# Weights laid out with the summed dimension first, a prologue without transposes, and x loaded by quarters

## The chip, the cores and the metric

The kernel runs on one NeuronCore of a Trainium2 chip. The core has five engines with a queue of instructions each: TensorE (PE in the profile; its weight loads are listed apart as PEld), VectorE (DVE), ScalarE (ACT), GpSimd (POOL) and SyncE (SP). They work side by side and wait for each other by semaphores. PE reads SBUF and writes PSUM; DMA moves data between HBM and SBUF. The metric is the device time of one execution in microseconds, median of several runs. Before the change it was 1078.87 us (three runs, 1078.11 to 1079.22).

## What is computed

```python
w = weights[conditions]                       # (128, 64, 64), one matrix for each of 128 samples
x1 = einsum('bct,bcd->bdt', x, w)             # x is (128, 64, 512)
h  = gelu(x1 @ ternarize(W1).T + b1)          # W1 is (2048, 512)
y  = h @ ternarize(W2).T + b2                 # W2 is (512, 2048)
scale = max(|y|) / 7 + 1e-8                   # over the whole tensor
out = x + clip(round(y / scale), -7, 7) * scale

def ternarize(W):
    delta = 0.05 * max(|W|)
    mask = |W| > delta
    return sum(|W| where mask) / max(sum(mask), 1) * sign(W) * mask
```

All arrays are float32, except for the conditions, which are integers.

## The kernel before

The 128 samples make 16 blocks (n = 0 to 15) of eight samples, that is 512 columns (samples times channels). Each block goes through two layers of 16 steps (hc = 0 to 15), one step for each 128 of the 2048 hidden units.

A block's input comes from "condition": the eight gathered 64x64 matrices stand in pairs on the diagonals of four 128x128 tiles ("diag"), and PE multiplies a pair of samples of x by each (`mix`, into PSUM tile "pc"). To keep float32 accuracy, a value is stored as a high and a low part, both in the format fp32r (`split`: ACT copies the high part, DVE or POOL subtracts to get the low one), and every product is made with both. The weights are ternary, -1, 0 or 1, so one part is enough. They are kept as fp8 in "w1t" and "w2t", and POOL widens 128x512 of them to fp32r ("wf") just ahead of use (`widen1`, `widen2`).

A step of layer 1 (`layer1`) is eight products of 128x512 into PSUM tile "ph". `bend` has ACT apply Gelu with scale alpha into a "ring" tile and splits the result into "h". A step of layer 2 (`layer2`) is eight products into the four PSUM tiles "py", which sum over all 16 steps. `result` then scales by the second alpha and keeps y in SBUF, and `largest` takes the maximum of it.

Blocks 2 to 11 (`SEVEN`) make layer 1 of two steps together with seven products of half size in place of eight (`seven`, driven by `pair`; weights combined once into "w1s"). `condition7` prepares their inputs with five intermediate results in a scratch tile "mixed". The other blocks go by `eight`. x of the next block is loaded on SP's queue: two DMAs of 512 KB into a "big" tile, at the first pair or step of the block ahead.

The prologue (block 0, and all that comes before) has to find the thresholds. In nat1 and nat2 the weights lie as they come from HBM, with the hidden unit or output channel on the partitions, so that the summed dimension lies along the row. DVE takes the maxima of W1, group by group (four groups of four steps), as they arrive. ACT makes signs and magnitudes. From the threshold on, DVE makes mask and sign of each group (`mask1`, `signed1`), and PE turns the ternary tiles (`turn1`, `turn2`: eight transposes of 128x128 in bf16 for two steps, into PSUM tile "pt"), ACT or DVE casts the result to fp8 into w1t or w2t, and POOL widens from there. `count1` counts the masks by products with a tile of ones, `alpha_1` joins the sums. Layer 1 of block 0 starts before alpha is known: `early` makes the products into five rotating PSUM tiles, `early_bend` follows four steps behind. Layer 2 of block 0 follows after all of its layer 1, and in between the four mixes of block 1. Fifty-two products of ones ("idle") keep PE busy until the first threshold.

Every engine runs its instructions in the order in which the program writes them (class `InOrder`); nothing rearranges them. Tiles come from pools: "big" has 20 tiles of 8 KB for each partition, "half" 10 of 4 KB. A tile that takes the place of another waits until that one's last reader is done.

At the end, when the maximum of all y is known, x is loaded once more, y is rounded, added to x and written out.

All lines of the kernel are recorded as line 54 in the profile (the class `InOrder` makes each instruction), so groups are told apart by their tiles' names.

Of the kernel before, what the change touches and what calls it, by code (L numbers as in the profile page):

```python
# [38 lines left out]
P = 128  # L40
# [17 lines left out]
def tile_cond_ternary_ffn(  # L58
# [17 lines left out]
    H = W1.shape[0]  # L76
    assert 2 * C == P and 2 * D == P and W1.shape[1] == T and C == D

    NT = T // P
    NH = H // P  # L80
# [7 lines left out]
    SEVEN = range(2, 12)  # L88
# [36 lines left out]
    first = big.tile([P, 5, max(B, P)], F32, tag="big", name="first")  # L125
    cond_i = first[:, 0, :B].bitcast(I32)
    sp.dma_start(out=cond_i, in_=conditions.partition_broadcast(P))
# [4 lines left out]
    PIECES.append([slice(0, 2), slice(2, 3), slice(3, GH)])  # L132
    for g in range(NG):
        w = big.tile([P, GH, T], F32, tag="big", name=f"nat1_{g}")
        rows1 = W1[g * GH * P : (g + 1) * GH * P, :].rearrange("(k p) t -> p k t", p=P)
        for ks in PIECES[g]:
            sp.dma_start(out=w[:, ks, :], in_=rows1[:, ks, :])
        nat1.append(w)
    x_next = load_x(0)
    b1n = first[:NH, 4, :P]  # L140
    sp.dma_start(out=b1n, in_=b1.rearrange("(k p) -> k p", p=P))
    for g in range(NG):
        w = big.tile([P, NT, GH * P], F32, tag="big", name=f"nat2_{g}")
        sp.dma_start(
            out=w,
            in_=W2[:, g * GH * P : (g + 1) * GH * P].rearrange("(i p) h -> p i h", p=P),
        )
        nat2.append(w)
# [4 lines left out]
    ident_b = const.tile([P, P], BF16)  # L153
    make_identity(nc, ident_b)
    ident_f = const.tile([P, P], F32)
    make_identity(nc, ident_f)
    ones_b = const.tile([P, P], BF16)
    pool.memset(ones_b, 1.0)
    ones_f = const.tile([P, P], F32)
    pool.memset(ones_f, 1.0)  # L160

# [8 lines left out]
    cond_f = first[:, 1, :B]  # L170
    dve.tensor_copy(cond_f, cond_i)
    wrap = first[:, 2, :B]
# [3 lines left out]
    cond_2 = cond_f.rearrange("p (j two) -> p j two", two=2)  # L176
# [4 lines left out]
    for h in range(2):  # L181
        dve.tensor_scalar(
            rows[half_of(h), :],
            cond_2[half_of(h), :, h],
            float(C),
            chan_f[half_of(h), :],
            ALU.mult,
            ALU.add,
        )
# [31 lines left out]
    def mix(xt, j, pc):  # L221

        for c in range(NT):
            pe.matmul(
                out=pc[:, c, :],
                lhsT=xt[j // 2][:, j % 2, c * P : (c + 1) * P],
                rhs=diag[:, j, :],
                start=True,
                stop=True,
            )  # L230

    def condition(n, j, xt, two):
        pc = ps_c.tile([P, NT, P], F32, tag="pc", name=f"pc_{n}_{j}")
        mix(xt, j, pc)
        split(pc, *(t[:, :, j * P : (j + 1) * P] for t in two))


    w1t = big.tile([P, NH, NT, P], F8, tag="big", name="w1t")
    w1t_f = w1t.rearrange("p h c k -> p h (c k)")
    w2t = big.tile([P, NH, T], F8, tag="big", name="w2t")  # L240

# [28 lines left out]
    def turn(dst, src, name):  # L270

        pt = ps_c.tile([P, len(src), NT, P], BF16, tag="pc", name=f"pt_{name}")
        for i, tiles in enumerate(src):
            for c, t in enumerate(tiles):
                pe.transpose(pt[:, i, c, :], t, ident_b)
        return lambda engine, dst=dst, i=slice(0, len(src)): (
            engine.copy(dst, pt[:, i], saturate=False)
            if engine is act
            else engine.tensor_copy(dst, pt[:, i], saturate=False)
        )  # L280

    def turn1(g, i, sign):

        hc = g * GH + 2 * i
        return turn(
            w1t[:, hc : hc + 2],
            [
                [sign[:, (2 * i + k) * T + c * P :][:, :P] for c in range(NT)]
                for k in range(2)
            ],  # L290
            f"1_{g}_{i}",
        )

    def turn2(g, i, sign):
        hc = g * GH + 2 * i
        return turn(
            w2t[:, hc : hc + 2].rearrange("p k (c d) -> p k c d", c=NT),
            [
                [sign[:, c * GH * P + (2 * i + k) * P :][:, :P] for c in range(NT)]
                for k in range(2)  # L300
            ],
            f"2_{g}_{i}",
        )

# [4 lines left out]
    signs = [big.tile([P, 2, WCH], BF16, tag="big", name=f"signs_{i}") for i in range(2)]  # L309
    junk = big.tile([P, 2, WCH], BF16, tag="big", name="junk")  # L310
# [3 lines left out]

    def sign1(g):
        act.activation(signs[g // 2][:, g % 2, :], flat(nat1[g]), AF.Sign)
# [14 lines left out]
    for _ in range(52):  # L331
        pe.matmul(out=idle, lhsT=ones_b, rhs=above[:, :T], start=True, stop=True)
# [17 lines left out]
    fetched = [fetch(1, j) for j in range(PAIRS)]  # L350
# [3 lines left out]
    def mix0(j):  # L354
        pc = ps_y.tile([P, NT, P], F32, tag=f"py{j}", name=f"pc_0_{j}")
        mix(x_next, j, pc)
# [14 lines left out]
    mix0(0)  # L371
    mix0(1)
    hi0(0)
    hi0(1)
    tern1 = {}

    def mask1(g, part=slice(0, WCH)):

        if g not in tern1:
            tern1[g] = big.tile([P, 2, WCH], BF16, tag="big", name=f"tern1_{g}")  # L380
        dve.tensor_scalar(
            tern1[g][:, 0, part], flat(mags[g])[:, part], delta1, None, ALU.is_gt
        )

    def signed1(g, part=slice(0, WCH)):
        both = tern1[g]
        dve.tensor_tensor(
            both[:, 1, part], both[:, 0, part], signs[g // 2][:, g % 2, part], ALU.mult
        )

    def count1(g, number, first, final):
        for i in range(WCH // T):
# [3 lines left out]
                rhs=tern1[g][:, 0, i * T : (i + 1) * T],  # L396
                start=(first and i == 0),
                stop=(final and i == WCH // T - 1),
# [9 lines left out]
    mask1(0, parts1[0])  # L408
    signed1(0, parts1[0])
    turned = turn1(0, 0, tern1[0][:, 1, :])  # L410
    lo0(0)
    lo0(1)
    mix0(2)
    mix0(3)
    pb = ps_c.tile([P, NH], F32, tag="pc", name="pb")
    pe.transpose(pb, b1n, ident_f[:NH, :NH])
    b1t = const.tile([P, NH], F32)
    wf1 = [half.tile([P, 2, NT, P], F32R, tag="half", name=f"wf1_{i}") for i in range(2)]
    w1f = [wf1[i // 2][:, i % 2] for i in range(4)]
    turned(act, w1f[0], 0)  # L420
    hi0(2)
    hi0(3)
    turned(act)
    sign1(3)
    lo0(2)
    lo0(3)
    mask1(0, parts1[1])
    signed1(0, parts1[1])
    dve.tensor_copy(b1t, pb)
# [4 lines left out]
    wide1 = {(0, 0): w1f[0]}  # L434
# [7 lines left out]
    def widen1(n, hc):  # L442

        w = w1f[hc % 4] if n == 0 else w1f[hc % 2]
        pool.tensor_copy(w, w1t[:, hc])
        wide1[n, hc] = w

    def widen2(n, hc):
# [7 lines left out]
        pool.tensor_copy(w, w2t[:, hc])  # L456
        wide2[n, hc] = w

    def layer1(n, hc, ph, pieces=1):

        w = wide1.pop((n, hc))
        for i in range(pieces):
            part = slice(i * BLK // pieces, (i + 1) * BLK // pieces)
            for c in range(NT):
                for k in range(2):
# [55 lines left out]
    rings = [half.tile([P, 2, BLK], F32, tag="half", name=f"ring_{i}") for i in range(2)]  # L521
    ring = [rings[i // 2][:, i % 2, :] for i in range(4)]

    def early(hc):
# [6 lines left out]
        layer1(0, hc, ph, 2 if hc == 0 else 1)  # L531
        waiting[hc] = ph

    def early_bend(hc):
        if hc % 2 == 0:
            pairs0[hc // 2] = big.tile([P, 2, 2, BLK], F32R, tag="big", name=f"h_{hc}")
        h = pairs0[hc // 2]
        bend(
            0,
            hc,  # L540
            waiting.pop(hc),
            [h[:, hc % 2, k, :] for k in range(2)],
            ring[hc % 4],
            pool if hc in (0, 2, 4, 6, 8, 12, 14) else dve,
        )

    def alpha_1():

        total = ps_c.tile([P, NG], F32, tag="pc", name="total1")
        pe.matmul(out=total, lhsT=ones_f, rhs=sums1, start=True, stop=True)  # L550
        count = const.tile([P, 1], F32, name="count1")
# [555 lines left out]
```

## Time and profile before

| what | us |
|---|---|
| median of three runs | 1078.87 |
| the profiled execution | 1079.13 |
| its span on the chip | 1077.4 |
| PE busy | 999.9 (93%) |
| PEld busy | 867.2 (80%) |
| DVE busy | 594.8 (55%) |
| ACT busy | 598.6 (56%) |
| POOL busy | 613.8 (57%) |
| first threshold known, first mask starts | 18.94 |
| alpha of W1 known, first Gelu starts | 40.78 |
| first product of layer 2 of block 0 | 67.6 |
| first product of block 1 | 100.64 |
| first block by seven products starts | about 163.8 |
| block 12 (eight products) starts | about 761.3 |

The span is the time between the first and the last instruction that the profiler recorded; the execution as timed is 1.7 us longer. A group's row gives engine, operation, tiles written and read, shape, and count, then busy time and mean duration of one in ns, then the engine's idle time ahead of these instructions and what ended it. A row of the timeline gives start, duration (of several merged instructions where "xN" says so), engine and operation, and in brackets the idle time before it. "PEclk" is the clock that TensorE was granted, as a share of full speed.

### The profile page before, as it was taken

How to read it: one execution, taken by the hardware profiler on the slowest of the kernel's cores; microseconds unless marked ns; L12 is line 12 of the kernel's file. 1: busy time of each engine (PE TensorE's matmuls, PEld its weight loads, DVE VectorE, ACT ScalarE, POOL GpSimd, SP SyncE). 2: the span in 40 equal slices, each digit the busy share in tenths (PEclk: the TensorE clock that was granted, in tenths of full speed). 3: DMA queues.
4: the chain of work that ended last, by engine and by line, in shares of the span. 5: the costliest groups of instructions: out<-in, count | busy, mean ns of one | idle time of the engine just before them, and what ended most of it. 6: DMA issues, size and time to landing. Idle time of an engine off the chain costs nothing.

```text
span 1077.4 us, 16522 instructions
## 1 busy us (share of the span) xinstructions
PE 999.9 (93%) x5778; PEld 867.2 (80%) x5780; DVE 594.8 (55%) x1035; ACT 598.6 (56%) x1010; POOL 613.8 (57%) x996
## 2 busy tenths in 40 slices
PE   7999999999999999999999999999999999999400
PEld 4778788999999999999999999999888888888300
DVE  6985845565665566665656556564423223231692
ACT  6865345666666565656656665665443443433481
POOL 4574836666676757666666667575534435333242
PEclk9999999999999999999999999999999999999855
DMA  9202010010100010010101000100200010041799
GB/s 326 87 17 101 5 40 5 2 43 3 42 4 2 5 41 5 1 44 2 43 4 41 5 1 6 40 5 2 82 2 2 4 40 6 1 145 32 283 413 376
DMA packets 28802, 62.22 MB, mean 58 GB/s; under 512 B 2848, under 2 KB 2992, under 8 KB 28720
## 3 DMA queue, kind: packets, MB, share of 16 engines
q1 hardware_dynamic: 22064, 42.28, 11.4%
q0 software_dynamic: 6656, 18.88, 4.5%
q8 instruction: 47, 0.77, 0.3%
q14 instruction: 35, 0.29, 0.1%
HBM read 44.38 MB, written 16.78 MB: 57 GB/s over the span
## 4 chain that ended last, share of the span: by engine, by line
PE 89%; DMA 5%; DVE 4%; ACT 1%; issue 1%; POOL 0%; SPq 0%; POOLq 0%; DVEq 0%; ACTq 0%
PE py L54 43%; PE ph L54 15%; PE xy L54 14%; PE z L54 11%; PE pc L54 5%; DMA xt<-in_x 3%; DVE top L54 1%; DMA out<-y 1%; DMA nat<-in_L_ffn_W 1%; DVE tern L54 1%; PE pt L54 1%; DVE y L54 0%; DVE h L54 0%; ACT ring L54 0%; ACT diag L54 0%
## 5 line engine op out<-in xcount | busy, mean ns | idle before, releaser
L54 PE MATMUL py<-wf,h 128*128 128x512 f32 x2048 | 530.6, 395 | 1.4 <-ACT h L54 0.7
L54 PEld LDWEIGHTS py<-wf,h 128*128 128x128 f32 x2048 | 366.2, 189 | 67.3 <-DVE y L54 2.3
L54 DVE TENSOR_TENSOR h<-ring,h 128x512 fp32r<-128x512 f32 x249 | 191.8, 771 | 227.9 <-ACT h L54 227.9
L54 POOL CAST wf<-w2t 128x512 fp32r<-128x512 fp8e4 x256 | 185.3, 726 | 176.2 <-PE py L54 160.6
L54 POOL CAST wf<-w1t 128x512 fp32r<-128x512 fp8e4 (+1 forms) x255 | 172.5, 682 | 78.0 <-PE ph L54 57.4
L54 PE MATMUL ph<-x,wf 128*128 128x512 f32 (+1 forms) x776 | 192.4, 391 | 1.8 <-POOL wf L54 0.7
L54 ACT ACTIVATE ring<-ring,b1t,alpha_w 128x512 f32<-128x512 f32 x160 | 131.2, 820 | 88.8 <-DVE ring L54 88.8
L54 POOL CAST wf<-w1s 128x256 fp32r<-128x256 fp8e4 (+1 forms) x240 | 122.2, 514 | 99.4 <-PE xy L54 72.7
L54 ACT ACTIVATE ring<-ph,b1t,alpha_w 128x512 f32<-128x512 f32 x96 | 74.9, 780 | 176.3 <-PE ph L54 174.7
L54 PEld LDWEIGHTS ph<-x,wf 128*128 128x128 f32 x776 | 144.5, 188 | 33.3 <-POOL wf L54 1.3
L54 ACT CAST h<-ring 128x512 fp32r<-128x512 f32 x256 | 158.9, 621 | 8.3
L54 DVE TENSOR_TENSOR ring<-xy,ring 128x256 f32<-128x256 f32 (+1 forms) x160 | 88.3, 552 | 58.9 <-PE xy L54 58.9
L54 PEld LDWEIGHTS xy<-xt,wf 128*128 128x128 f32 x640 | 97.8, 189 | 12.8
L54 PE MATMUL xy<-xb,wf 128*128 128x256 f32 x640 | 101.9, 281 | 0.0
L54 PE MATMUL xy<-xt,wf 128*128 128x256 f32 x640 | 101.7, 282 | 0.0
L54 PEld LDWEIGHTS xy<-xb,wf 128*128 128x128 f32 x640 | 92.7, 190 | 7.1
L54 ACT COPY ring<-xy 128x256 f32<-128x256 f32 x160 | 59.1, 370 | 61.6 <-PE xy L54 61.6
L54 PE MATMUL z<-xt,wf 128*128 128x256 f32 x640 | 89.4, 282 | 0.0
L54 ACT COPY ring<-z 128x512 f32<-128x512 f32 x80 | 47.0, 588 | 66.9 <-DVE h L54 63.7
L54 PEld LDWEIGHTS z<-xt,wf 128*128 128x128 f32 x640 | 82.0, 190 | 0.0
L54 POOL DMA_INDIRECT wg<-in_L_cond_weights,rows x64 | 72.3, 1130 | 13.8 <-issue 5.4
L54 DVE TENSOR_TENSOR xt<-mixed,xt 128x512 fp32r<-128x512 f32 x40 | 30.7, 767 | 81.8 <-ACT xt L54 81.8
(111 smaller groups left out, 825.6 us busy)
## 6 DMA issues: line engine op xcount, KB each, us to landing
xt<-in_x SPq DMA_DIRECT2D x60, 512.0 KB, 5.2
out<-y POOLq DMA_DIRECT2D x30, 512.0 KB, 12.8
nat<-in_L_ffn_W SPq DMA_DIRECT2D x6, 1024.0 KB, 14.7
nat<-in_L_ffn_W SPq DMA_DIRECT2D x3, 512.0 KB, 11.4
wg<-in_L_cond_weights,rows POOLq DMA_INDIRECT x64, 2.6
w1t<-in_x SPq DMA_DIRECT2D x4, 256.0 KB, 2.6
w2t<-in_x SPq DMA_DIRECT2D x4, 256.0 KB, 2.7
out<-xt POOLq DMA_DIRECT2D x2, 512.0 KB, 8.5
```

Of the source, the lines that this page charges most:

```text
L54: return lambda *args, **kw: self._tc.keep_in_program_order(make(*args, **kw))
```

## The change

It does five things. The host hands over W1, W2, b1 and the conditions in another layout (`LAID_OUT`), with the summed dimension on the partitions, so that `turn`, `turn1` and `turn2` with their transposes and casts are gone. The order of the prologue is written anew: block 0's widenings read the ternary bf16 tiles ("terns") directly; w1t and w2t are made later, during layer 2 of block 0, by ACT (`kept`). Six ring tiles in place of two let the low halves of odd steps wait (`low`). x of the blocks by seven, and of the block behind them, comes by quarters of 256 KB into a "half" tile with two places, which `condition7` also uses for its intermediate results. And block 12 goes by seven products too. The load of the conditions moves from SP's queue to ACT's, a first use of Gelu on one column stands ahead of everything on ACT, and there are 54 idle products in place of 52.

```diff
-    SEVEN = range(2, 12)
+    SEVEN = range(2, 13)
...
-    sp.dma_start(out=cond_i, in_=conditions.partition_broadcast(P))
+    act.dma_start(out=cond_i, in_=conditions)
...
-        rows1 = W1[g * GH * P : (g + 1) * GH * P, :].rearrange("(k p) t -> p k t", p=P)
         for ks in PIECES[g]:
-            sp.dma_start(out=w[:, ks, :], in_=rows1[:, ks, :])
+            sp.dma_start(out=w[:, ks, :], in_=W1f[:, g * GH :, :][:, ks, :])
...
+    sp.dma_start(out=b1t, in_=b1)
...
+        sp.dma_start(out=w, in_=W2[:, g * GH : (g + 1) * GH, :])
...
-    def turn(dst, src, name):
...
-                pe.transpose(pt[:, i, c, :], t, ident_b)
...
+        if n == 0:
+            w = w1f[hc % 4]
+            g, i = divmod(hc, GH)
+            pool.tensor_copy(flat(w), group1(terns, g)[:, i * T : (i + 1) * T])
...
+        on_pool = hc % 2 == 0 and hc < NH - 2
+        bend(0, hc, waiting.pop(hc), two, ring[hc % len(ring)], pool if on_pool else None)
...
+    fetched = [fetch(1, 0)]
+    mask1(0, parts1[0])
+    signed1(0, parts1[0])
+    widen1(0, 0)
     widen1(0, 1)
+    lo0(0)
+    lo0(1)
+    hi0(2)
+    hi0(3)
+    lo0(2)
+    lo0(3)
+    fetched += [fetch(1, 1)]
     early(0)
+    early(1)
+    mask1(0, parts1[1])
+    signed1(0, parts1[1])
+    widen1(0, 2)
+    widen1(0, 3)
+    fetched += [fetch(1, j) for j in range(2, PAIRS)]
+    abs1(3)
+    for g in range(NG - 1):
+        above1(g)
+    sign1(3)
...
+    early(3, lambda: next(find, None))
+    signed1(2)
     widen1(0, 5)
     early(4)
     early_bend(0)
+    widen1(0, 6)
...
+    def behind(hc):
+        if 5 <= hc < 5 + NG:
+            largest2(hc - 5)
+        if 6 <= hc < 6 + PAIRS:
+            place(hc - 6, fetched[hc - 6])
+        if hc == 9:
+            signed1(3)
+        if hc == 11:
+            delta.extend(next(find))
+            signed2(0)
+        if hc == 12:
+            low(0, 1)
+            low(0, 3)
+            signed2(1)
         if hc == 14:
+            widen2(0, 0)
         if hc == 15:
+            widen2(0, 1)
...
+        if hc + 2 < NH:
+            widen1(0, hc + 2)
         early_bend(hc - 4)
         behind(hc)
...
+    def kept(t, g, tiles):
+        act.copy(flat(t[:, g * GH : (g + 1) * GH]), group1(tiles, g), saturate=False)
...
+        if hc == 0:
+            signed2(2)
+        if hc == 1:
+            for i in (13, 14, 15):
+                low(0, i)
+        if hc < NG:
+            kept(w1t, hc, terns)
+        if hc == 3:
+            signed2(3)
...
+                count2(g)
+            else:
+                kept(w2t, g, terns2)
+        if hc in (5, 7, 9, 11):
+            j = (hc - 5) // 2
+            condition(1, j, pair_of(x_next, j), two_next)
+            sum2(j)
...
-        t, b12 = extra["t"], extra["b12"]
+        t = xp.rearrange("p (a c d) -> p a c d", a=4, c=2)
+        b12 = t[:, 3]
...
+    def quarter_x(n, j):
+        sp.dma_start(out=extra["x"][:, j % 2, :], in_=x_blk[n][:, j, :])
...
-                    x_next.append(load_x(n + 1))
...
+                if k == 1:
+                    quarter_x(n + 1, 0)
+                    quarter_x(n + 1, 1)
+                if k in (4, 5):
+                    quarter_x(n + 1, k - 2)
...
+LAID_OUT = {
+    "itok_B_1_198": lambda a: a.reshape(-1, 2).T.repeat(P // 2, axis=0),
+    "L0_ffn_W1": lambda a: a.reshape(-1, P, a.shape[1] // P, P).transpose(3, 0, 2, 1),
+    "L0_ffn_b1": lambda a: a.reshape(-1, P).T,
+    "L0_ffn_W2": lambda a: a.reshape(a.shape[0], -1, P).transpose(2, 1, 0),
+}
```

## The prediction

> **What bounds the kernel now.** I read the busy shares first (PE 93%), then the chain that ended last (PE 89% of it), then busy time by stage. Columns: stretch, its length, busy time of PE, PEld, DVE, ACT and POOL with instruction counts, granted PE clock, DMA share, GB/s.
>
> ```profile
> 0.00:20.00 20.00, 15.10 (x68) 7.45 (x69) 12.76 (x21) 12.90 (x8) 9.86 (x28) 1.00 0.90 309
> 20.00:40.00 20.00, 17.91 (x110) 13.50 (x111) 15.46 (x19) 16.25 (x17) 8.87 (x16) 0.91 0.68 246
> 40.00:62.00 22.00, 20.58 (x113) 15.83 (x111) 21.20 (x22) 18.26 (x26) 14.91 (x13) 1.00 0.01 2
> 62.00:73.00 11.00, 10.14 (x65) 8.07 (x64) 8.99 (x8) 9.52 (x14) 8.27 (x8) 1.00 0.01 1
> 73.00:101.00 28.00, 27.70 (x162) 22.80 (x163) 19.68 (x16) 14.69 (x17) 15.41 (x15) 1.00 0.23 83
> 101.00:163.80 62.80, 62.73 (x292) 51.25 (x291) 35.85 (x60) 27.32 (x48) 35.79 (x48) 1.00 0.10 33
> 163.80:223.60 59.80, 59.80 (x386) 54.37 (x386) 35.46 (x75) 34.98 (x69) 39.66 (x68) 1.00 0.01 3
> ...
> 761.30:823.00 61.70, 61.70 (x289) 51.35 (x288) 19.92 (x31) 25.79 (x38) 26.85 (x44) 1.00 0.07 20
> ```
>
> From 101 us on PE is hardly ever idle: a block by seven products lasts 59.8 us (163.8 to 223.6), one by eight with its four mixes 61.7 (block 12). After PE's end near 1010 us comes a tail that the change leaves alone. So two things can move the time: the kind of block 12, and the moment at which block 1 starts on PE, 100.64 us. Ahead of that moment PE has work that it keeps from 18.15 us on: eight mixes of 0.98 (two took 1.96), 16 first products of 1.81, 14 second products of 1.81 and some 4 us of counting, 66 us in 82.5. The rest is transposes, waits and a lowered clock (0.91 in 20 to 40).
>
> **Part 1, the transposes go.** Both matrices arrive with the summed dimension on partitions.
>
> ```profile
> L54 PE MATMUL pt<-ident_b,tern 128*128 128x128 bf16 x128 | 10.2, 224 | 1.1 <-DVE tern L54 1.1
> L54 ACT CAST w2t<-pt 128x1024 fp8e4<-128x1024 bf16 x8 | 8.1, 1010 | 11.0 <-PE pt L54 11.0
> L54 ACT CAST w1t<-pt 128x1024 fp8e4<-128x1024 bf16 x7 | 7.1, 1008 | 2.9 <-PE pt L54 2.9
> ```
>
> Sixteen groups of eight transposes go. A group holds PE for 0.40 us (one starts at 65.27, the next product at 65.67), so 6.4 us of path. The chain transpose, ACT cast, POOL cast becomes one POOL cast from bf16; 16 casts leave ACT's and DVE's queues. Eight ACT casts of 2048 columns come in ("kept"). 512 columns took 0.59, 1024 took 1.01, so some 1.87 each, 15 us, now during the second products, where ACT was busy 14.7 of 28 us. With counts at 1.9 + 0.2 their last starting mix copy is ready at about 91 us by my sum, just ahead of its use. A bf16 to fp32r cast on POOL is not in the trace: between 0.61 (the same from fp8, shortest) and 0.81 (mean of the first weights' casts). I take 0.62, nearest in shape; the upper end is at most 3 us on the path.
>
> **Part 2, the first loads.** The index load leaves SP's queue for ACT's: SP issued it at 0.75 and the first weights at 1.19, so 0.44 us earlier. ACT's wait for the first weights covers its issue (idle 5.8 us). DVE's maxima follow the first arrival without a gap, so the threshold comes near 18.4 instead of 18.9. b1 comes as 64-byte rows; it is used 20 us later, which hides it. The rows of weights are 8 KB long, 32 KB apart; see the slower rival.
>
> **Part 3, alpha.** DVE in its new order from 18.4: mask and sign of half a group (1.6), four low halves (0.69 each, held by ACT's copies until 22.4), so 23.1; other half 1.7; mask and sign of group 1 2.5; two masks 2.6; the masked sum 2.3: 32.2. In this stretch POOL issues four widenings and three gathers, and these take turns with DVE.
>
> ```profile
> 40.59 0.16 DVE L54 TENSOR_TENSOR alpha_w<-kept,count 128x1 f32<-128x1 f32 x1
> 40.78 0.78 ACT L54 ACTIVATE ring<-ph,b1t,alpha_w 128x512 f32<-128x512 f32 x1 [1.50 <-DVE alpha_w L54]
> ...
> 58.72 2.34 DVE L54 SCALAR_TENSOR_TENSOR tern<-nat,delta_w,tern 128x2048 bf16<-128x2048 f32 x1
> 59.09 3.13 POOL L54 TENSOR_TENSOR h<-ring,h 128x512 fp32r<-128x512 f32 x1 [3.44 <-ACT h L54]
> ...
> 60.98 2.80 DVE L54 TENSOR_TENSOR h<-ring,h 128x512 fp32r<-128x512 f32 x2
> ...
> 62.16 2.09 POOL L54 CAST wf<-w1t 128x512 fp32r<-128x512 fp8e4 x2
> ...
> 63.29 2.14 PE L54 MATMUL ph<-x,wf 128*128 128x512 f32 x8 [0.68 <-POOL wf L54]
> ...
> 100.64 1.98 PE L54 MATMUL ph<-x,wf 128*128 128x512 f32 x8
> ```
>
> The POOL subtraction beside DVE's 2.34 us takes 3.13 instead of 1.29: it only works once DVE is done (61.06 + 1.2). The two DVE subtractions behind it take 2.80 instead of 1.4. A gather issued beside a 2.70 us DVE addition (117.46) took 2.84 instead of 1.0. The Trainium skill (SBUF — State Buffer, "SBUF: two separate sides") says that DVE and GpSimd share one pair of ports which the first holds for its whole instruction. The rows agree; what the rule alone forbids is adding only the longest engine. By durations alone alpha would come at 34.4; with turns (three to four POOL operations of 0.6 to 1.0 in between) the sum ends at 35.3, eight small steps bring alpha at 37.4. Before: 40.75. ACT's second table load (1.28 at 38.01) goes too, worth nothing: ACT waited 1.5 for alpha behind it. The total for alpha now sits in the middle of product 3 on PE: up to 1.2 us of wait there.
>
> **Part 4, the first products.** The first Gelu ends at 38.2 and frees the PSUM bank of product 5; PE has finished product 4 at the same time. ACT needs 1.33 us a step (40.78, 42.12, 43.45), PE 1.81, so PE leads. Eleven products make 19.9; product 6 waits 0.7 (its widening stands behind POOL's first subtraction, 38.85 + 1.3 + 0.6 = 40.75), the second threshold's transpose costs 0.35. That would be 59.2. Then from 50.9 DVE's two ternarizations of W2 (1.29 + 2.34 each) and two low halves take turns with POOL's widenings 13 to 15 and two subtractions: the widening of product 15 ends at 58.4, so product 15 ends at 60.2. The first W2 widening stands behind them all: 62.3 if POOL takes the first turn, 64.6 if DVE does. I take 62.3, because POOL is free 0.1 us earlier. Layer 2 of block 0 started at 67.4.
>
> **Part 5, the second products.** 14 of 1.81 and four mixes of 0.9 to 0.98 make 29.1, plus 1 us for turns at widenings 2 and 3: block 1 starts at 92.4, 8.2 us earlier. x of block 1 is loaded once block 0's inputs are dead (about 60); 512 KB took 5.2, its first use is at 74: hidden by six products; if it weren't, at most that load's 5 us.
>
> **Part 6, x by quarters.** Four loads of 256 KB instead of two of 512 on SP's queue. SP now waits inside a block for a quarter's buffer; only later x loads are behind it, and the next are used a block later. The quarter is also condition7's scratch, so it comes free when that pair's split ends.
>
> ```profile
> 257.67 0.74 DVE L54 TENSOR_TENSOR xt<-mixed,xt 128x512 fp32r<-128x512 f32 x1 [2.39 <-ACT xt L54]
> ...
> 258.88 1.06 PE L54 MATMUL pc<-diag,xt 128*128 128x128 f32 x8
> ...
> 266.81 1.06 PE L54 MATMUL pc<-diag,xt 128*128 128x128 f32 x8
> ```
>
> Pair 0's quarter is free at 258.41, pair 2's mix is due at 266.81: 8.4 us, for an issue of 0.4 and a landing of 2.6 (the row of 256 KB loads of x). 5.4 us are left. In block 1 the mixes are 4.5 us apart (132.81, 137.34) and the split ends at 137.53; there 1.4 us are left. Taken at nothing; bounds 0 and 2 us.
>
> **Part 7, block 12 by seven.** 61.7 minus 59.8: 1.9 us, all on PE's path. Its extra vector work lies under PE, as in ten blocks before.
>
> **The sum.** Profiled span 1077.4 - 8.2 - 1.9 = 1067.3; that execution took 1079.1, 1.7 around the span, so 1069.0. The median is 0.3 lower: 1068.8.
>
> **The rivals.**
>
> A. The turns are cheaper than I sum (POOL slips in while DVE waits). Then PE alone counts: alpha at 35.5, layer 2 at 57.5, block 1 at 86.6, 14 us earlier: 1063. For it: three of the waits are mine, not measured. Against: every overlap in the rows above was paid in full. 0.22.
>
> B. The turns cost more: DVE first, widenings of layer 2 also late. Block 1 at 95 to 97, total 1071.5 to 1075. For it: POOL's queue is in order, so one late subtraction holds all widenings. 0.20.
>
> C. Slower than before: the weights come slowly. The Trainium skill (DMA: Bandwidth & Descriptors, "Latency and other measured facts") tells of row pitches at large powers of two: at 512 KiB 207 GB/s. This change makes the pitch of both matrices 32 KB; before, W1 was read in whole megabytes and W2 at a pitch of 8 KB, both at 360 to 410 GB/s. By the rows W1's 4.19 MB take some 11 us, by an estimate at the page's 207 they take 20.3: 9.5 us later for the threshold, and everything behind it; that cancels nearly all of the gain of 10.1. It decides below 200 GB/s; at 150 (28 us) the time would be 1086. 8 KB is the nearer row (two doublings against four), so I take the full rate. Slower: 0.05; a rate that leaves about nothing: 0.03.
>
> D. Quarters arrive late. Price: two late quarters in each of 11 blocks. A landing of 8 us instead of 2.6 would be needed to begin with. The DMA share in those blocks is 0.01 to 0.1. It would need 0.5 us each to cancel the gain. Under 0.01.
>
> **How the numbers follow.** Mine 0.50, 1066 to 1071.5; A 0.22; B 0.20; C 0.08. Cases of one sign hold most; the range runs from 1063 (A) to 1075 (B). Faster by over 0.2% (2.2 us, about what a measurement of this kernel can tell from no change) 0.92, within 0.03, slower 0.05.
>
> **What would show it.** No transposes in the list; alpha near 37.4; product 15 ending near 60; the first py product near 62; block 1 near 92; every seven-product block still 59.8 with no PE wait on x; block 12 at 59.8; the rate in the first 25 us near 390 GB/s. I am wrong if the first weights land after 9 us, if POOL's casts from bf16 take over 0.9, or if PE waits for a quarter.

## The result and the profile after

The changed kernel took 1067.61 us (median of four, 1066.95 to 1069.97) beside 1078.49 of the kernel before on the same chip: a ratio of 0.9903, 95% interval 0.9892 to 0.9915. Five more executions of it, made later beside the last experiment, gave 1069.37 (1067.48 to 1071.19), ratio 0.9920 (0.9906 to 0.9933). The prediction was 1068.8, in a range of 1063 to 1075, and faster with a chance of 0.92. Both sets lie inside the range, but its single steps were right less often than its sum.

In the profiled execution the span fell from 1077.4 to 1067.9 us, by 9.5. This execution, 1069.97 us, was the slowest of the first four; the spans of the other three were 1065.1 to 1066.1. Read from PE's rows: block 1 starts 8.31 earlier, block 12 is 2.05 shorter, blocks 1 to 11 together are 0.31 longer, the tail behind PE's last stage is 0.54 longer.

Busy time by stage of the kernel after, columns as in the prediction:

```profile
0.00:20.00 20.00, 15.87 (x67) 7.41 (x68) 12.61 (x21) 13.31 (x9) 8.40 (x22) 1.00 0.93 357
20.00:40.00 20.00, 19.17 (x116) 15.04 (x115) 18.64 (x23) 15.51 (x18) 15.48 (x17) 1.00 0.36 144
40.00:60.00 20.00, 18.26 (x80) 14.35 (x78) 18.29 (x15) 17.15 (x27) 19.51 (x22) 1.00 0.17 54
60.00:72.00 12.00, 10.43 (x39) 8.45 (x40) 11.96 (x10) 9.52 (x8) 12.00 (x9) 0.86 0.14 44
...
91.00:153.50 62.50, 62.48 (x290) 51.02 (x289) 37.41 (x61) 25.92 (x46) 37.94 (x48) 1.00 0.07 19
...
753.10:812.90 59.80, 59.80 (x385) 54.38 (x384) 31.88 (x53) 35.62 (x62) 37.01 (x66) 1.00 0.11 34
```

PE's clock is now 1.00 in 20 to 40 (0.91 before) and 0.86 in 60 to 72 (1.00 before). POOL is busy for 19.51 of 20 us from 40 on; time in which one of its instructions is held up counts as busy. Block 12 has the length and the shape of a seven-product block.

Rows of the timeline of the kernel after, for the marks that the prediction named:

```profile
6.10 0.20 DVE L55 CAST first<-first 128x64 f32<-128x64 int32 x1 [4.03 <-DMA first<-in_itok_B]
7.21 9.04 DVE L55 TENSOR_REDUCE top<-nat 128x1 f32<-128x2048 f32 x7
17.84 0.81 DVE L55 TENSOR_SCALAR masks<-nat,delta_w 128x1024 bf16<-128x1024 f32 x1
18.16 1.16 PE L55 MATMUL pc<-diag,xt 128*128 128x128 f32 x8 [0.94 <-POOL diag L55]
...
35.94 0.78 ACT L55 ACTIVATE ring<-ph,b1t,alpha_w 128x512 f32<-128x512 f32 x1 [2.99 <-issue]
36.91 8.86 DVE L55 TENSOR_REDUCE top<-nat 128x1 f32<-128x2048 f32 x4
38.70 1.73 POOL L55 CAST wf<-terns 128x512 fp32r<-128x512 bf16 x3
42.22 0.61 POOL L55 CAST wf<-terns 128x512 fp32r<-128x512 bf16 x1
...
57.79 3.27 DVE L55 SCALAR_TENSOR_TENSOR terns<-nat,delta_w,junk 128x2048 bf16<-128x2048 f32 x1
58.85 3.69 POOL L55 CAST wf<-terns 128x512 fp32r<-128x512 bf16 x2
61.58 12.78 PE L55 MATMUL py<-wf,h 128*128 128x512 f32 x48 [2.74 <-POOL wf L55]
92.33 1.98 PE L55 MATMUL ph<-x,wf 128*128 128x512 f32 x8
```

PE has done product 15 (the last step of layer 1) at 58.84 and waits 2.74 us for the first weights of layer 2. POOL widens them beside DVE's ternarization of 3.27 us: two casts of 0.61 take 3.69.

### The profile page after: what moved, and what is told of

It reads as the page before. It is cut to its first block, busy times and chain, and to the rows that moved or that the text cites. A ratio compares the mean times of both kernels' runs of the same rounds, so it can differ in the third digit from the quotient of the medians.

```text
span 1067.9 us, 16731 instructions
## 1 busy us (share of the span) xinstructions
PE 991.2 (93%) x5765; PEld 866.0 (81%) x5765; DVE 613.4 (57%) x1080; ACT 610.0 (57%) x1038; POOL 635.3 (59%) x1019
## 4 chain that ended last, share of the span: by engine, by line
PE 88%; DMA 3%; POOL 3%; DVE 2%; ACT 1%; issue 1%; SPq 1%; POOLq 0%; DVEq 0%; ACTq 0%
PE py L55 44%; PE xy L55 16%; PE z L55 12%; PE ph L55 11%; PE pc L55 5%; DMA xt<-in_x 2%; POOL wf L55 2%; DVE y L55 1%; ACT diag L55 1%; POOL wg L55 1%; POOL h L55 1%; SPq L55 1%; DMA wg<-in_L_cond_weights,rows 1%; DMA first<-in_itok_B 0%; POOL diag L55 0%
## 5 line engine op out<-in xcount | busy, mean ns | idle before, releaser
L55 POOL CAST wf<-w2t 128x512 fp32r<-128x512 fp8e4 x242 | 174.4, 721 | 151.7 <-PE py L55 147.7
L55 ACT ACTIVATE ring<-ring,b1t,alpha_w 128x512 f32<-128x512 f32 x176 | 144.4, 820 | 97.7 <-DVE ring L55 97.7
L55 POOL CAST wf<-w1s 128x256 fp32r<-128x256 fp8e4 (+1 forms) x264 | 133.8, 511 | 109.8 <-PE xy L55 80.6
L55 POOL CAST wf<-w1t 128x256 fp32r<-128x256 fp8e4 (+1 forms) x240 | 157.1, 659 | 56.3 <-PE ph L55 45.3
L55 PE MATMUL ph<-x,wf 128*128 128x512 f32 (+1 forms) x648 | 158.5, 389 | 1.1 <-POOL wf L55 1.0
L55 ACT ACTIVATE ring<-ph,b1t,alpha_w 128x512 f32<-128x512 f32 x80 | 62.3, 779 | 145.5 <-PE ph L55 141.9
L55 PEld LDWEIGHTS ph<-x,wf 128*128 128x128 f32 x648 | 119.7, 188 | 27.9 <-POOL wf L55 3.0
L55 PE MATMUL xy<-xb,wf 128*128 128x256 f32 x704 | 112.4, 282 | 0.0
L55 PE MATMUL xy<-xt,wf 128*128 128x256 f32 x704 | 111.8, 282 | 0.0
L55 DVE TENSOR_TENSOR xt<-x_quarters,xt 128x512 fp32r<-128x512 f32 x44 | 33.8, 768 | 91.0 <-ACT xt L55 91.0
```

Of the source, the lines that this page charges most:

```text
L55: return lambda *args, **kw: self._tc.keep_in_program_order(make(*args, **kw))
```

## The experiments

All edits are to the changed kernel. Times are medians with the lowest and the highest execution, ratios are against the kernel before on the same chip. "Products of ones" are products that nobody uses and that only keep PE busy.

**Block 12 back to eight products.**

```diff
-    SEVEN = range(2, 13)
+    SEVEN = range(2, 12)
```

> The changed kernel with Part 7 alone undone: block 12 makes eight products again. Mine: block 12 lasts 61.8 instead of 59.8, nothing else moves, so 1.9 to 2.1 us more than the changed kernel: about 1069.6, ratio to the kernel before 0.992. Rival: the extra vector work of a seven-product block 12 (or the load of x for block 13) costs something behind it, so that undoing it adds less than 1 us.

Measured: 1071.3 (1068.99 to 1071.95), ratio 0.9933. In the trace:

```profile
751.10:812.90 61.80, 61.80 (x289) 51.48 (x288) 20.01 (x31) 25.79 (x38) 26.77 (x44) 1.00 0.06 20
```

The block takes 61.88 us between its first product and that of the next block (751.07 to 812.95), against 59.81 with seven (753.10 to 812.91): 2.07. Part 7 stands. The median lies 3.7 over the changed kernel's first set and 1.9 over its second; why one kernel's sets differ by 1.8 is shown further below. The profiled span, 1067.2, is even shorter than the changed kernel's 1067.9: in this execution PE's clock stayed at 1.00 behind the same wait, so that layer 2 lasted 29.24 us (60.98 to 90.22) instead of 30.75.

```profile
60.98 11.27 PE L55 MATMUL py<-wf,h 128*128 128x512 f32 x48 [2.71 <-POOL wf L55]
```

**Weights without the long pitch.** The host lays each group of four steps out as one megabyte, rows of 8 KB at a pitch of 8 KB.

```diff
-            sp.dma_start(out=w[:, ks, :], in_=W1f[:, g * GH :, :][:, ks, :])
+            sp.dma_start(out=w[:, ks, :], in_=W1[g][:, ks, :])
...
-        sp.dma_start(out=w, in_=W2[:, g * GH : (g + 1) * GH, :])
+        sp.dma_start(out=w, in_=W2[g])
```

> Each group of W1 and W2 is laid out as one contiguous megabyte: rows of 8 KB at a pitch of 8 KB instead of 32 KB, all else the changed kernel. Mine: no difference, first 20 us at 357 GB/s as with 32 KB, first mask at 17.8, same time within 0.2%. Rival C in a small form (the 32 KB pitch costs some of the rate): more GB/s in the first 20 us, the last W1 piece earlier; each us of it moves the threshold by up to 1 us.

Measured: 342 GB/s in the first 20 us (357 with the long pitch), DVE's maxima from 7.19 (7.21), layer 2 at 61.64, block 1 at 92.36: every mark is within 0.1 us of the changed kernel's. The profiled span was 1067.8 against 1067.9. The median, 1070.45 (1069.44 to 1071.9), lies 2.8 above the changed kernel's first median and 1.1 above its second; that the times are the same within 0.2% is shown by the marks, not by the medians. A pitch of 32 KB costs nothing here, and rival C falls.

**The index load back on SP's queue.**

```diff
-    act.dma_start(out=cond_i, in_=conditions)
+    sp.dma_start(out=cond_i, in_=conditions)
```

> The index load alone goes back to SP's queue, ahead of the weights. In the changed kernel the index lands at 6.0, beside the first weights (5.9), and DVE, which has its five index steps first, starts the maxima at 7.2. If DVE is what then sets the threshold (maxima without a gap, 9.04 us of them), the index lands at about 4.4 again, the maxima start at 6.4 with the weights 0.44 later, and the first mask comes 0.8 us earlier, at 17.0; the gathers are issued at 6.4 instead of 7.6, so the diagonal tiles no longer hold the first mixes (1.2 us). First product of layer 1 at about 21.4 instead of 22.6, alpha near 35.0; but the start of layer 2 hangs on the turns of DVE and POOL behind the second threshold, so the end moves 0 to 1 us: 1066.6 to 1067.6. Rival (the move of the index load is worth its 0.44, as Part 2 had it): threshold 0.4 later, end 0.4 later.

Measured: 1066.85 (1065.8 to 1068.45), ratio 0.9887. The timeline:

```profile
2.58 0.39 DVE L55 CAST first<-first 128x64 f32<-128x64 int32 x1 [0.52 <-DMA first<-in_itok_B]
6.09 2.29 DVE L55 TENSOR_REDUCE top<-nat 128x1 f32<-128x2048 f32 x1 [2.12 <-DMA nat<-in_L_ffn_W]
17.23 0.27 PE L55 MATMUL tops_delta_w<-ident_f,first 128*128 128x128 f32 x1
17.34 3.74 PE L55 MATMUL pc<-diag,xt 128*128 128x128 f32 x32
18.13 0.74 DVE L55 TENSOR_SCALAR masks<-nat,delta_w 128x1024 bf16<-128x1024 f32 x1
...
59.97 6.21 PE L55 MATMUL py<-wf,h 128*128 128x512 f32 x20 [2.74 <-POOL wf L55]
```

Issued ahead of the weights, the 32 KB land by 2.58; issued on another queue at the same moment as the first megabyte, they landed at 6.1. The diagonals are ready, the first product starts at 20.84 instead of 22.57, layer 2 1.6 earlier. The threshold, though, comes 0.3 later, not 0.8 earlier: my expectation missed that PE's 54 products of ones run to about 17.2 and the threshold's transpose stands behind them.

**The same with 48 products of ones.** Besides the index load on SP's queue:

```diff
-    for _ in range(54):
+    for _ in range(48):
```

> The index load on SP's queue ahead of the weights, as in the run before, and 48 products of ones instead of 54 at the start. In the run before DVE had the maxima ready at 15.9, but PE's products of ones ran to 17.2 and the threshold's transpose stood behind them. With 48 they end at 15.6: the first mask at 16.8 instead of 18.1 (17.8 in the changed kernel), the first product of layer 1 at about 19.6, alpha at about 33, layer 2 at 58.5 to 59, that is 1.2 earlier than with the index load alone; time 1065 to 1066. Rival: the gap between the last product of ones and the mixes lowers the clock, or the port chain behind the second threshold takes the gain back: no better than 1066.8.

Measured: first mask at 17.00, first product 19.71, alpha 32.95, layer 2 at 58.82, all as expected; but 1066.84 (1065.36 to 1067.2), ratio 0.9897, not the 1065 to 1066 hoped for. PE still waits 2.71 us ahead of layer 2, and the clock falls behind it (0.73, 0.50 and 0.92 in three stretches of 2 us from 58). The rival's figure is what is measured. Neither of its reasons holds as it was put: behind the products of ones the clock stays at 1.00, and the port doesn't take the gain back. Profile against profile, each with one such fall, layer 2 is 1.15 us earlier than with the index load alone, and block 1 still 0.9 (89.58 instead of 90.49). The mean clock of each execution points to the fall: 0.970 for the one at 1065.36, 0.968 or 0.969 for the other three.

**PE's gap filled.** Nine products of ones stand behind product 15.

```diff
+    filler = ps_c.tile([P, T], F32, tag="pc", name="filler")
+    for _ in range(9):
+        pe.matmul(
+            out=filler, lhsT=ones_b, rhs=group1(terns, 0)[:, :T], start=True, stop=True
+        )
```

> The changed kernel with nine products of ones (512 columns, 0.26 us each, 2.4 us in all; their result is used by nobody) behind product 15 of layer 1, in the gap in which PE waits 2.74 us for the first weights of layer 2. Theory (the half-speed stretch of 3.4 us, granted clock 0.58 and 0.57 in 62 to 66, comes of that gap; some executions of the changed kernel have it and some don't, which is its spread of 1067 to 1070): no stretch below 1.00 before the tail, layer 2 still starts at 61.0 to 61.6, block 1 at 90.3 to 90.7 instead of 92.3, times 1066 to 1067.3, all close together. Rival (the clock falls for another reason): still a half-speed stretch in the profile, or a spread of 3 us as before.

Busy time by stage, first of the changed kernel, then of this run:

```profile
62.00:64.00 2.00, 2.00 (x7) 1.58 (x6) 2.00 (x3) 2.00 (x3) 2.00 (x2) 0.58 0.41 99
64.00:66.00 2.00, 2.00 (x6) 1.53 (x6) 2.00 (x3) 2.00 (x2) 2.00 (x3) 0.57 0.46 163
```

```profile
62.00:64.00 2.00, 2.00 (x10) 1.60 (x10) 2.00 (x2) 2.00 (x2) 2.00 (x3) 1.00 0.56 156
64.00:66.00 2.00, 2.00 (x10) 1.53 (x9) 2.00 (x3) 2.00 (x2) 2.00 (x3) 1.00 0.28 107
```

PE makes ten products in 2 us instead of seven and six. Layer 2 starts nearly as late as ever (61.25), block 1 at 90.50 instead of 92.33. All four executions took 1067.69 to 1067.94. The median (1067.85, ratio 0.9909) is no better than the changed kernel's first one: the fill doesn't beat an execution in which the clock holds, it makes all of them hold.

**The changed kernel once more.**

> The changed kernel once more, with more executions, beside the last version on one chip. Theory: its times fall into two groups some 1.7 to 2.8 us apart, by whether the clock falls to half for 3.4 us behind the gap ahead of layer 2 of block 0: 1066.8 to 1067.3 without and 1068.5 to 1070 with. Against it: all times alike.

Measured: 1067.48, 1069.00, 1069.37, 1069.61 and 1071.19. They are not two groups but a ladder, and the mean clock falls along it: 0.970 for the shortest, 0.969 for the next two, 0.968, and 0.967 for the longest. The longest is the profiled one, and it has two half-speed stretches:

```profile
16.00:24.00 8.00, 6.35 (x38) 5.91 (x38) 4.30 (x11) 4.74 (x6) 5.54 (x11) 0.79 1.01 416
...
62.00:64.00 2.00, 1.36 (x5) 1.17 (x6) 2.00 (x3) 2.00 (x2) 2.00 (x3) 0.91 0.00 0
64.00:66.00 2.00, 2.00 (x6) 1.52 (x6) 2.00 (x3) 2.00 (x2) 2.00 (x2) 0.50 0.88 258
```

Of three profiles with the same work around them, none, one and two stretches went with spans of 1065.8 (filled), 1067.9 and 1069.1, steps of 2.1 and 1.2. By the clock each stretch costs 1.7 us (8 us at 0.79, or 2 us each at 0.58 and 0.57).

**Dummy groups in place of the transposes.** Eight groups of eight small products, in one run in layer 1, in the other in layer 2 of block 0 (the last three lines in place of the two before them).

```diff
+    def dummy(name):
+        pt = ps_c.tile([P, 4, P], F32, tag="pc", name=name)
+        for i in range(8):
+            pe.matmul(out=pt[:, i % 4, :], lhsT=ones_b, rhs=ones_b, start=True, stop=True)
...
+        if hc < 13:
+            dummy(f"pt_{hc}")
...
+        if 1 <= hc <= 4:
+            dummy(f"pt_{hc}")
+            dummy(f"pu_{hc}")
```

> Eight groups of eight 128x128 bf16 products go into layer 1 of block 0, one group ahead of each of products 5 to 12, as dear for PE as the transposes of W1 were (0.40 us a group, 3.2 in all); nobody uses them. As the prediction summed (each group lies on PE's path): layer 2 of block 0 and all behind it 3.2 later, layer 2 at 64.8. Rival: PE's waits in that stretch (0.44, 0.58 and 2.74 us) take them up, since the first weights of layer 2 are made behind the turns of DVE and POOL: product 15 ends 2 to 3 later, layer 2 starts at 61.6 to 62.2, the end moves by 0 to 0.6.

> The same eight groups, but in layer 2 of block 0, two ahead of each of its steps 1 to 4. PE does not wait in this stretch of the changed kernel once it has started, so both views expect the full 3.2 us there: layer 2 to block 1 lasts 32.4 instead of 29.2 (30.8 where the clock falls), the end 3.2 later, about 1070.8. Only if POOL's widenings were what sets these steps would it be less than 1.5.

Measured in layer 1: 1069.45 (1068.59 to 1070.96), ratio 0.9929. In layer 2: 1073.26 (1071.18 to 1073.76), ratio 0.9953. Timeline of the first, then of the second:

```profile
60.37 5.98 PE L55 MATMUL py<-wf,h 128*128 128x512 f32 x25
90.98 0.47 PE L55 MATMUL ph<-x,wf 128*128 128x512 f32 x1 [1.28 <-ACT x L55]
```

```profile
68.02 0.62 PE L55 MATMUL pt<-ones_b 128*128 128x128 bf16 x8
68.48 0.61 PE L55 MATMUL pu<-ones_b 128*128 128x128 bf16 x8
68.90 2.08 PE L55 MATMUL py<-wf,h 128*128 128x512 f32 x8
70.83 0.62 PE L55 MATMUL pt<-ones_b 128*128 128x128 bf16 x8
96.39 1.98 PE L55 MATMUL ph<-x,wf 128*128 128x512 f32 x8
```

A group holds PE for 0.44 us (68.02 to 68.90 for two). With the step of layer 2 behind them, two groups take 2.81 us (68.02 to 70.83) where the step alone takes 1.81, so a group costs 0.50 there. In layer 1 eight of them, at least 3.5 us, do not make layer 2 start later (60.37), and there is no wait ahead of it now. They take the place of PE's waits. One of these waits also goes because the turns fall otherwise: with PE later, POOL widens the first weights of layer 2 (done at 59.11) ahead of the long part of DVE's second ternarization (60.23), not beside it. What the groups cost, 0.5 us at the start of block 1 and 1.0 from block 2 on, against the run with the gap filled, comes through ACT: its casts to w1t begin at 61.91 instead of 59.90, and its last mix copy of block 1 at 90.24 instead of 88.94. The medians lie 1.6 apart where the profiled spans lie 0.8 apart; that rest was not traced. In layer 2 the eight groups cost 4.06 us (block 1 at 96.39 against 92.33, with one half-speed stretch in either run): full price, and more than the 3.2 expected, because a group costs 0.50 and not 0.40.

**DVE's order alone.**

```diff
         if hc == 12:
-            low(0, 1)
-            low(0, 3)
+            for i in (1, 3, 5, 7):
+                low(0, i)
+        if hc == 15:
+            low(0, 9)
+            low(0, 11)
             signed2(1)
...
-    for hc in (5, 7, 9, 11):
-        low(0, hc)
```

> Only DVE's order is changed: six low halves (0.7 us each) go ahead of the second ternarization of W2 (1.6 and 3.3 us) instead of two ahead of it and four behind. The same instructions, the same POOL queue. Mine (POOL waits for a port that DVE holds for its whole instruction): widening 15 and the first two widenings of layer 2 stand beside short DVE work, so PE's waits of 0.58 and 2.74 us go and layer 2 starts at about 58.6 instead of 61.6; the widening of step 4 is then due at 65.8, with group 1 ready at about 63.5. End 2.5 to 3.3 us earlier, 1064.3 to 1065.1, if nothing behind gives it back. Rival 1 (POOL's own queue sets the start, its durations are its own work): no change, layer 2 at 61.6. Rival 2: the later group 1 holds widening 4, and the gain is given back there, under 1 us in the end.

Measured: 1067.83 (1067.32 to 1068.12), ratio 0.9898. The timeline:

```profile
58.25 2.10 POOL L55 CAST wf<-terns 128x512 fp32r<-128x512 bf16 x2
59.38 3.92 PE L55 MATMUL py<-wf,h 128*128 128x512 f32 x16 [0.61 <-POOL wf L55]
61.98 12.99 POOL L55 CAST wf<-terns 128x512 fp32r<-128x512 bf16 x8
63.16 2.58 DVE L55 SCALAR_TENSOR_TENSOR terns<-nat,delta_w,junk 128x2048 bf16<-128x2048 f32 x1
63.65 2.11 PE L55 MATMUL py<-wf,h 128*128 128x512 f32 x8 [0.35 <-POOL wf L55]
66.27 3.93 PE L55 MATMUL py<-wf,h 128*128 128x512 f32 x16 [0.51 <-POOL wf L55]
```

The same two casts on the same POOL take 2.10 instead of 3.69, and only DVE's work beside them is another: 0.7 us long instead of 3.3. So POOL's time was DVE's, and rival 1 falls. But the end is rival 2's: the ternarization comes later, the next eight casts take 12.99 us (10.86 in the run with the filled gap), PE waits at steps 2, 3 and 5, and block 1 starts at 90.55, where the run with the filled gap has it (90.50). Moving a collision doesn't remove it.

**Three subtractions from POOL to DVE**, besides that order.

```diff
-        on_pool = hc % 2 == 0 and hc < NH - 2
+        on_pool = hc % 2 == 0 and hc < 8
...
-            low(0, 1)
-            low(0, 3)
+            for i in (1, 3, 5, 7, 8):
+                low(0, i)
+        if hc == 15:
+            for i in (9, 10, 11):
+                low(0, i)
             signed2(1)
...
-    for hc in (5, 7, 9, 11):
-        low(0, hc)
...
-            for i in (13, 14, 15):
+            for i in (12, 13, 14, 15):
```

> The changed kernel with DVE's order as in the run that put six low halves ahead of the second ternarization, and three subtractions (low halves of steps 8, 10 and 12) moved from POOL (1.29 us each alone, 1.73 beside DVE) to DVE (0.69). Theory (in 50 to 75 DVE and POOL share one port, and their times add up: in the run with the order alone the start won 2.2 us and POOL's eight widenings, 12.99 us for 8 of 0.61, gave them back): 5.2 us of POOL's time go, DVE gets 2.1, 1.8 to 3.1 us less behind one another, so layer 2 starts at 58.4 to 59 with hardly a wait behind it, block 1 at 88 to 89, no fall of the clock, time 1065.5 to 1066.3. Rival (POOL's own queue alone counts): the start is earlier, but PE waits for widenings 4 to 9 as before, block 1 at 90.5, time 1067.8 as with the order alone.

Measured: 1067.51 (1066.73 to 1068.49), ratio 0.9906: no better. The timeline:

```profile
50.89 1.29 DVE L55 TENSOR_SCALAR junk<-nat,minus_w 128x2048 bf16<-128x2048 f32 x1
51.01 9.34 POOL L55 CAST wf<-terns 128x512 fp32r<-128x512 bf16 x7
59.14 7.41 PE L55 MATMUL py<-wf,h 128*128 128x512 f32 x32
65.84 8.19 POOL L55 CAST wf<-terns 128x512 fp32r<-128x512 bf16 x6 [5.49 <-DVE terns L55]
67.40 2.11 PE L55 MATMUL py<-wf,h 128*128 128x512 f32 x8 [0.85 <-POOL wf L55]
90.57 0.47 PE L55 MATMUL ph<-x,wf 128*128 128x512 f32 x1 [0.29 <-ACT x L55]
```

This execution lost 1.7 us to a half-speed stretch at 18 to 24, so everything starts late. From the second threshold's ternarization on, layer 2 starts after 8.25 us (50.89 to 59.14); in the changed kernel after 11.99 (49.59 to 61.58), with the order alone after 9.86. The port is relieved; now POOL idles 5.49 us for the second ternarization, which I had put behind eight low halves, and PE then waits for the casts behind it, and for ACT at block 1. Without the stretch at half speed block 1 would be at 88.9 by an estimate (90.57 less 1.7), the late end of what the theory had. The theory's time, 1065.5 to 1066.3, was missed all the same: the other three executions, with mean clocks of 0.970 and 0.971, took 1066.73 to 1067.76. The time stayed near the rival's, but not for the rival's reason: as far as this trace shows, the bound had gone to DVE's order, which neither had named.

**Early index and filled gap together.** The edits of three runs above: index load on SP's queue, 48 products of ones, nine more in the gap.

> The index load on SP's queue first, 48 products of ones at the start, and the nine products of ones in PE's gap ahead of layer 2 of block 0. Theory (the gap makes the clock fall in most executions, the early index gives some 2.5 us): no stretch below 1.00 before the tail; layer 2 at 58.8, block 1 at 87.8 instead of 89.6 (with the fall) or 90.5 (filled, without the early index); all runs within 1 us of each other, spans at 1063.2 to 1063.6, times 1065.2. Rival: what the fill saves the clock it costs elsewhere: 1066 to 1067.

Measured: 1065.37 (1065.06 to 1065.63), ratio 0.9890; layer 2 at 58.74, block 1 at 88.00, no stretch below full clock ahead of the tail, spans 1063.2 to 1063.8.

**All together**, without the filled gap: the early index, 48 products of ones and the three subtractions, with the ternarization behind five low halves, and `count2`'s output put where ACT's next cast writes. Its old scratch, "junk", is read by a ternarization of DVE, and ACT waited for that (2.48 us ahead of 70.00 and 1.41 ahead of 77.28 in the changed kernel). The lines that are new:

```diff
...
+        if hc == 15:
             signed2(1)
+            for i in (9, 10, 11):
+                low(0, i)
...
-            junk[:, g % 2, :], group2(g), AF.Square, accum_out=sums2[:, 1, g : g + 1]
+            flat(w2t[:, g * GH : (g + 1) * GH]),
+            group2(g),
+            AF.Square,
+            accum_out=sums2[:, 1, g : g + 1],
+            saturate=False,
```

> Index load on SP's queue first, 48 products of ones at the start, three subtractions moved from POOL to DVE, the second ternarization of W2 behind five low halves and ahead of three, and the counts of W2 written to w2t instead of to the scratch that DVE's next ternarization reads (ACT waited 1.55 and 4.00 us for that). Theory (port, then ACT's wait, are what is left between the second threshold and block 1): second threshold at 47 (from 49.6), layer 2 at 55.3 to 56, no wait longer than 0.5 behind it, block 1 at 85 to 86.5; 1.5 to 3 us better than the version with early index and filled gap: 1062.5 to 1064. Rival: PE waits for widenings 4 to 9 or for ACT's last copies as before, block 1 at 88, time 1065 or more.

Measured: 1062.29 (1062.07 to 1063.24), ratio 0.9862 (0.9847 to 0.9877), beside 1069.37 of the changed kernel on the same chip. The timeline, and then all of PE's waits from 15 to 95 us (sum, times, longest):

```profile
46.78 1.29 DVE L55 TENSOR_SCALAR junk<-nat,minus_w 128x2048 bf16<-128x2048 f32 x1
55.01 11.04 PE L55 MATMUL py<-wf,h 128*128 128x512 f32 x48
84.03 1.98 PE L55 MATMUL ph<-x,wf 128*128 128x512 f32 x8
```

```profile
PE tops_delta_w L55 <- DVE first L55: 0.6, 1, 0.6
PE ph L55 <- POOL wf L55: 0.4, 1, 0.4
PE ph L55 <- DVE x L55: 0.3, 1, 0.3
```

1.3 us of waits are left of 5.2, and there is no half-speed stretch. Block 1 starts 8.3 earlier than in the changed kernel. This is faster than both kernels. How much of the last 3.1 us (1062.29 against 1065.37, on two chips) belongs to the subtractions, to the place of the ternarization and to the counts was not taken apart.

## Why the prediction was right

**Part 1, half wrong.** No transpose is left, POOL's cast from bf16 takes 0.61 where DVE doesn't hold it up (0.62 taken; the mean of all 30 is 1.14), ACT's casts of 2048 columns 1.89 in the mean (1.87), the last starting mix copy is at 89.33 (91). The step that failed is "so 6.4 us of path". The dummy groups, put into the changed kernel, show it: layer 2's half is path at full price, 4 us and not 3.2, while layer 1's half costs 0.5 to 1.0, since PE waits there anyway. The sum was not hurt, because it never subtracted the 6.4; it added forward from alpha through the turns.

**Part 2, one term mis-sized, one missed.** The first mask is at 17.84 (18.4 predicted, 18.94 before). The first weights were used from 5.92 instead of 7.84, 1.9 us sooner where I had 0.44, as ACT's first rows before and after show:

```profile
7.84 1.91 ACT L54 ACTIVATE signs<-nat 128x2048 bf16<-128x2048 f32 x1 [5.82 <-DMA nat<-in_L_ffn_W]
```

```profile
5.92 1.91 ACT L55 ACTIVATE signs<-nat 128x2048 bf16<-128x2048 f32 x1 [3.24 <-DMA nat<-in_L_ffn_W]
```

The first 20 us moved 357 GB/s instead of 309 (370 in the first 25, where I had near 390). Why the weights land so much sooner was not taken apart: with the index load back ahead of them they are used at 6.09, so its move is worth little. The rows of W1 in HBM went from 2 KB to 8 KB, and the index from 64 KB to 32; no run changes either alone. Against that stands what I had called a gain: the index load beside the weights lands at 6.05, DVE's five index steps hold its maxima to 7.21, and the diagonals hold the mixes. Layer 1 began at 22.57 (23.13 before). Putting the load back first made layer 1 begin at 20.84, and layer 2 1.6 us earlier.

**Part 3, turns overpriced.** Alpha came at 35.9 (37.4). From the first mask to the end of the masked sum it took 15.4 us, where I had 16.9. POOL's last two gathers waited, 2.24 and 2.72 us instead of 1.0, and DVE's operations grew only from 1.27 to 1.63 where POOL slipped in between. DVE paid 1.6 us over the 13.8 of its durations, with its waits for late mixes among them, not 3.1. The small steps behind it took 0.5 more than I had. PE waited 0.3 us for the total (up to 1.2 expected).

**Part 4, right.** Product 15 ended at 58.84 (60.2), layer 2 started at 61.58 (62.3; 64.6 at the other end). Product 15 is 1.4 earlier, about as much as alpha (1.5); layer 2 only 0.7, for from the second threshold's ternarization to its start it took 11.99 us where I had 11.4. The mechanism, widenings behind the turns of two ternarizations, is the one that the run with DVE's order shows, by 3.69 against 2.10 for the same two casts. The rule of the Trainium skill (SBUF — State Buffer, "SBUF: two separate sides") also says that a DVE operation takes the shared ports only with two inputs in SBUF or in a two-port mode, and this agrees: beside DVE's four maxima (36.91 to 45.77, one input each) POOL's three casts took 1.73 together and its subtractions 1.30 each, nothing extra.

**Part 5, right by luck.** Block 1 started at 92.33 (92.4), because three errors cancel. Layer 2 started 0.7 earlier than summed. The 1 us for turns at the widenings was not there: where the clock held, layer 2 with its mixes lasted 29.25 (gap filled) and 29.24 us (block 12 by eight), against my 29.1 and 1. And the half-speed stretch, which no step had, added 1.5 (30.75 in the changed kernel's profile). The kernel before had such a stretch too in its profiled execution, the 0.91 in 20 to 40 of the prediction's first table, so that it drops out of the difference of the two spans. I had named that lowered clock as a part of what isn't work, and given the changed kernel none. Two of the first four executions had spans of 1065.1, where the sum had 1067.3.

**Part 6, right.** A quarter lands in 2.6 us (median). In 150 to 990 us PE waits for nothing at all.

**Part 7, right.** Block 12 is 2.07 us shorter (1.9).

**The rivals.** A (turns cheaper, 1063) was nearly true of alpha (35.9 against its 35.5) and not of layer 2, where PE waited 2.74 for them; taken as a bound on what PE alone needs it was good, since with most of the turns, the late index load and ACT's scratch out of the way the kernel ran at 1062.3. B (1071.5 to 1075) is not the median, but one execution in nine, 1071.19, came near it, by the clock and not by turns. C and D did not happen. C had also read its row wrongly: the Trainium skill (DMA: Bandwidth & Descriptors, "Latency and other measured facts") gives 207 GB/s at 512 KiB for copies, in each direction, beside 214 for a padded pitch, which it calls full; its slow rates begin at 2 MiB, with 164. No run here has such a pitch.

## What to carry to other kernels

A cost removed from an engine is worth its time only where that engine isn't waiting: look for the wait behind it first, and add forward through the chain that ends last, as a difference of busy times would have claimed some 3 us too much here (layer 1's half of the 6.4). Where two engines share a port, put short operations beside each other and take work off the pair; moving the long one only moves the wait. And a gap on TensorE can cost twice, once as a wait and again in the clock behind it; nine useless products in the gap made all four executions alike, within 0.25 us.

## What the runs showed of the hardware

**Half speed behind short gaps.** The clock of PE fell to 0.50 for some 3.4 us (0.58 and 0.57 in two stretches of 2 us are 3.4 us at half) behind the wait of 2.7 us ahead of layer 2. It did so in six of the seven profiles of the changed kernel and its variants that have that wait, and there in none of the six in which it is filled or at most 0.8. It also fell at 18 to 24 us in two profiles, behind single waits of 0.2 to 1.5 us; others with a wait of 1.5 us there kept 1.00. And it fell at 26 to 31 in the kernel before, behind waits of 0.3 to 0.6. The Trainium skill (TensorE: Matmul & The Clock Gate, "Part 1: The HAM clock gate") has the clock halve after an idle window of about 3.4 us, with windows that run free of the kernel. The length agrees with these traces, and so does it that the same wait is followed by a fall in some executions only. That the idle time must be as long as the window does not agree: here less than 3 us was enough. How much idle time within a window is enough, these runs don't tell.

**A small load beside a large one.** The 32 KB of the index landed 1.8 us after their issue when they went first on SP's queue, and 5.3 us after it when they were issued on ACT's queue at the moment at which SP issued the first megabyte of weights. In the kernel before, 64 KB first on SP's queue took 3.7.
